# A list schedule's clock: other times from engine to engine, and a PSUM tile taken whole

## The chip, the cores and the metric

The kernel runs on one core of a Trainium2 chip. Five queues work side by side: PE (TensorE, matmuls and transposes), DVE (VectorE), ACT (ScalarE), POOL (GpSimd) and SP (which issues the DMAs). Each takes its instructions strictly in the order of the program; between queues only waits hold the order. The metric is device time in microseconds for one execution, lower is better. A time here is the median of several executions; the profile comes from one execution of its own.

## What is computed

Two sequences of 1024 positions and 128 channels go through four residual blocks, each behind a layer norm:

```python
x = x + mamba(_layernorm(x))       # selective state space, 256 inner channels, 16 states
x = x + experts(_layernorm(x))     # 8 experts, two picked one after the other, then a norm
x = x + encoder(_layernorm(x))     # 6 layers, below
x = x + fp4_ffn(_layernorm(x))     # gate, up, down with 4-bit blocks of 16
```

A layer of the encoder has 16 heads of 8 channels, and takes most of the time:

```python
scores = jnp.einsum('blhd,bmhd->bhlm', q, k) * inv_sqrt_d
w_avg = jax.nn.softmax(scores, axis=-1).mean(axis=1)           # mean over the heads
new_w = jax.nn.softmax(CSCALE * w_avg + rel[None], axis=-1)
sa = jnp.einsum('blm,bme->ble', new_w, h)
h1 = _ln(h + sa, l1w, l1b)
h2 = _ln(h1, l2w, l2b)
ff = jax.nn.relu(h2 @ w1.T + b1_) @ w2.T + b2_
return (_ln(h2 + ff, l3w, l3b), None)
```

## The kernel before

**The work.** Class `Front` holds the state space block and the experts, `Encoder` the six layers, `Last` the 4-bit block. In `Encoder.attention` a layer and a sequence are eight blocks of 128 query rows with 16 heads each, so 6 x 2 x 8 x 16 = 1536 heads in all. For one head, PE writes scores of 128 rows by 1024 keys into a PSUM tile `sc` (four matmuls, two on each half of the rows of the array), DVE takes their maximum (`nm`), ACT the exponential with its row sum (`e`, `z`). For four heads together DVE takes the reciprocals of the sums (`rz`), POOL multiplies each `e` by its own, and PE transposes `e` onto two PSUM accumulators (`acc0`, `acc1`; 16 small matmuls a head). After 16 heads ACT makes the second softmax (`prT`) from the accumulators, PE multiplies it with the hidden state (again in a tile `sc`), and DVE adds the residual into `r`.

There are three `sc` tiles of 128 x 1024 fp32 and fourteen `e` tiles. The same three `sc` tiles serve every other product of the encoder: the transposes before a projection, the projection, and the feed-forward part. `Encoder.between` does what lies between two attentions, for half a sequence (512 rows) at a time, so 24 calls. Its first feed-forward product is 512 hidden units by 512 rows: two `sc` tiles, each filled in two halves of 512 columns, and after each half's matmul a relu on ACT reads that half. A matmul of this kind is two instructions in the trace. The second product (`w2T`) fills one more tile.

**The order.** Nothing runs while it is written down: `Recorder` passes each call to `Plan.record`, which keeps it as an `Op` with its engine, an estimated cost and the earlier operations that it depends on. These come from the boxes of the tiles that it reads and writes (`View.box`, a range in each dimension): two operations depend on each other where their boxes meet and one of them writes. Calls under `together` are one `Op`.

`Plan.schedule` is a list scheduler with a clock of its own. An operation is ready (`arrive`) when all that it depends on has ended, plus a hop where the other one is on another engine; where it needs a new tile, not before a tile has been free for `GAP`. In each round every engine takes, among its ready operations that could start within `PATIENCE` = 0.1 us of the soonest, the one of the lowest key; of these the earliest over all engines is placed. The keys are positions in the chain of heads. Scores have a key 40 heads ahead of their place, so PE prefers them wherever they can start in time. The work of `between` is spread over the heads of the attention behind it (`Work.spread`): an operation may not be placed before the heads have reached its `late`, and those that use a PSUM tile already taken carry the key of that tile's first user less 4.

The order of these placements is the order in which the program's instructions are written, so it is the order in each queue, SP's included. The waits between engines are put in afterwards by the framework, from the real tiles and the written order. The clock of the scheduler is not part of the program.

One thing besides the order comes from that clock: where PE stands still for more than `STILL` = 0.3 us while accumulators are open, pairs of matmuls on zeros are written into the gap, one for each `ZEROS` = 0.22 us of it.

The costs are figures in `Plan.estimate`: 1.09 us for an exponential with its sum, 0.07 + 0.00104 a column for a maximum (1.135 us), 0.44 for the scores of a head, 0.50 for its 16 transposes.

Of the kernel before, what the change touches and what calls it, by code (L numbers as in the profile page):

```python
# [16 lines left out]
PSUM = bass.MemoryType.PSUM  # L17
# [80 lines left out]
class View:  # L98
# [23 lines left out]
    def rearrange(self, *args, **kw):  # L122
        return self._then("rearrange", *args, **kw)

    def of(self, n):

        return View(self.buf, self.chain, self.box, n)
# [93 lines left out]
def meet(a, b):  # L221
    return all(x[0] < y[1] and y[0] < x[1] for x, y in zip(a, b))
# [9 lines left out]
class Plan:  # L232
# [1 line left out]

    GAP = 0.06
    SWITCH = 0.12

    def __init__(self, nc):  # L240
# [14 lines left out]
    def record(self, engine, fn, name, args, kw):  # L255
        if self.group is not None and self.group.calls:
            o = self.group
            assert o.engine == engine
        else:
            o = self.group or Op()  # L260
            o.engine, o.calls, o.cost, o.deps, o.bufs = engine, [], 0.0, set(), []
            o.key, o.late, o.locks, o.rows = self.key + self.ahead, self.late, False, 128
            o.pos, o.sums = self.key, None
            o.i, o.start, o.after, o.landing = len(self.ops), None, [], 0.0
            self.ops.append(o)
        o.calls.append((fn, args, kw))
        outs = [args[0]] if args else [kw["out"]]
        if not isinstance(outs[0], View):
            outs = []
        ins = list(args[1:]) + [v for k, v in kw.items() if k not in ("out", "accum_out")]  # L270
        if "accum_out" in kw:
            outs.append(kw["accum_out"])
        outs = [v for v in outs if isinstance(v, View)]
        ins = [v for v in ins if isinstance(v, View)]
        for v in ins:
            o.deps.update(d for box, d, w in v.buf.touched if w and meet(box, v.box))
        for v in outs:
            o.deps.update(d for box, d, w in v.buf.touched if meet(box, v.box))
        for v in ins:
            v.buf.touched.append((v.box, o, False))  # L280
        for v in outs:
            covers = lambda x: all(a[0] <= b[0] and b[1] <= a[1] for a, b in zip(v.box, x[0]))
            v.buf.touched = [x for x in v.buf.touched if x[1] is o or not covers(x)]
            v.buf.touched.append((v.box, o, True))
        o.deps.discard(o)
        for v in outs + ins:
            if v.buf not in o.bufs:
                o.bufs.append(v.buf)
                v.buf.uses += 1
        self.estimate(o, engine, name, args, kw, outs, ins)  # L290
        return o
# [114 lines left out]
    def schedule(self, regions):  # L406
# [17 lines left out]
        def arrive(o):  # L424
            t = 0.0
            for d in o.deps:
                if d.engine == "SP":
                    x = d.end + d.landing
                elif d.engine != o.engine:
                    x = d.end + self.GAP + (0.13 if d.engine == "PE" else 0.05)  # L430
                else:
                    x = d.end
                t = max(t, x)
            o.ready = t
            ready[o.engine].append(o)

        for o in ops:
            if not o.waits:
                arrive(o)
        heads = [o for o in ops if o.late is None and o.engine != "SP"]  # L440
        front = 0
        n, moved, sums = 0, 0.0, ()
        while n < len(ops):
# [5 lines left out]
            for e in engines:  # L449
                found, soonest = [], None  # L450
                for o in ready[e]:
# [4 lines left out]
                    for b in o.bufs:  # L456
                        if b.at is None:
                            s = b.slots
                            if not s.free or s.ordered and s.bufs[0] is not b:
                                ok = False  # L460
                                break
                            t = max(t, min(s.free)[0] + self.GAP)
                    if not ok:
# [8 lines left out]
                if not found:  # L472
                    continue
                t, o = min(
                    ((t, o) for t, o in found if t <= soonest + self.PATIENCE),
                    key=lambda x: (x[1].key, x[1].i),
                )
# [3 lines left out]
            t, o = best  # L481
# [29 lines left out]
            for x in o.after:  # L511
                x.waits -= 1
                if not x.waits:
                    arrive(x)
        for r in regions:
            r.open()
        for o in order:
# [9 lines left out]
            else:  # L527
                self.issue(o)

    PATIENCE = 0.1  # L530
    STILL = 0.3
    ZEROS = 0.22
# [1445 lines left out]
```

## Time and profile before

| | |
|---|---|
| median of 3 runs | 3137.64 us (3136.42 to 3147.6) |
| the profiled execution's own time | 3140.7 us |
| its span, first to last instruction | 3138.9 us |
| mean granted TensorE clock | 0.962 |
| scores, maxima and exponentials of the encoder | from about 433 to 2995 us |
| exponentials (ACT) | 1536 of 1115 ns, plus 198 ns to read the sum (overlapping) |
| maxima (DVE) | 1536 of 1213 ns |
| scaling of `e` (POOL) | 1536 of 1122 ns |
| scores (PE) | 6144 matmuls |
| zero matmuls (PE) | 1518, 229.8 us |

In the profile a line of the timeline has a start, a length, the engine, the operation, the tile that it writes and those that it reads, how many were merged into the line, and in brackets how long the engine stood idle before it and who ended that wait. Lengths of matmuls are modelled, and overlap the next ones. A line of the waits has the waiting engine and tile, the one that ended the wait, the total in us, the number of waits and the longest. In the view by stretches each engine has its busy time and its instructions, and behind them stand the granted TensorE clock, the DMA engines' busy share and GB/s. All instructions have the same source line, that of the helper that issues them, so groups go by tile.

### The profile page before, as it was taken

What the parts mean: (1) busy time and instruction counts of PE and PEld (TensorE: products, weight loads), DVE (VectorE), ACT (ScalarE), POOL (GpSimd) and SP (SyncE); (2) the same over time, 40 slices, a digit from 0 to 9 for tenths busy, and PEclk for the clock granted to TensorE, in tenths of its full rate; (3) what the DMA queues carried; (4) which work ended last, traced back from release to release, by engine and by line L of the source; (5) the groups of instructions that cost most, each with busy time, mean ns of one, the idle gap of its engine ahead of it and who ended that gap; (6) DMA issues with size and microseconds to landing.
All of it is one profiled execution on the core that took longest, in us unless ns stands there. A gap on an engine that the chain in (4) does not pass through costs nothing.

```text
span 3138.9 us, 92400 instructions
## 1 busy us (share of the span) xinstructions
PE 2855.5 (91%) x38448; PEld 1940.4 (62%) x38448; DVE 2333.2 (74%) x3462; ACT 2486.8 (79%) x4461; POOL 2538.2 (81%) x2886
## 2 busy tenths in 40 slices
PE   6699999999999999999999999999999998999965
PEld 3455444566666666666666766666667666666643
DVE  4777533588778878787787877877777778778867
ACT  5577556688889888898888888888888888779843
POOL 5888634588889898898898988989898799788845
PEclk8699999999999999999999999999999999999986
DMA  4233321023032231221322303223023132220000
GB/s 137 99 108 110 88 69 39 23 62 86 25 85 55 61 95 29 73 68 45 79 55 62 77 25 95 59 55 85 25 72 82 30 81 55 51 63 25 17 3 12
DMA packets 209427, 193.42 MB, mean 62 GB/s; under 512 B 127778, under 2 KB 174446, under 8 KB 205550
## 3 DMA queue, kind: packets, MB, share of 16 engines
q1 hardware_dynamic: 209006, 187.51, 22.9%
q8 instruction: 300, 4.92, 0.7%
q14 instruction: 121, 0.99, 0.1%
HBM read 129.52 MB, written 57.93 MB: 60 GB/s over the span
## 4 chain that ended last, share of the span: by engine, by line
PE 47%; ACT 22%; DVE 13%; issue 4%; POOL 3%; DMA 1%; SPq 0%; DVEq 0%; ACTq 0%; POOLq 0%
PE sc L404 26%; ACT e L404 16%; PE acc L404 14%; DVE nm L404 9%; PE ps L404 3%; PE po L404 3%; ACT prT L404 2%; POOL e L404 2%; ACT r L404 2%; PE acc L524 1%; DVE st L404 1%; DVE fh L404 1%; DVE r L404 1%; DMA k<-d_k 1%; ACT ff L404 1%
## 5 line engine op out<-in xcount | busy, mean ns | idle before, releaser
L404 DVE TENSOR_REDUCE nm<-sc 128x1 f32<-128x1024 f32 x1536 | 1800.3, 1213 | 439.6 <-PE sc L404 400.3
L404 POOL TENSOR_SCALAR e<-e,rz 128x1024 f32<-128x1024 f32 x1536 | 1690.9, 1122 | 267.9 <-DVE rz L404 262.7
L404 ACT ACTIVATE e<-sc,nm 128x1024 f32<-128x1024 f32 x1536 | 1704.6, 1115 | 212.1 <-DVE nm L404 137.5
L404 PEld LDWEIGHTS acc<-ident,e 64*128 64x128 f32 x24576 | 973.2, 141 | 207.4 <-POOL e L404 39.0
L404 PE MATMUL sc<-k,q 36*128 36x512 bf16 x6144 | 914.5, 380 | 85.1 <-ACT e L404 58.4
L404 PE MATMUL acc<-ident,e 64*128 64x64 f32 x24576 | 984.0, 225 | 6.7 <-issue 5.4
L404 PEld LDWEIGHTS <-q 36*128 36x128 bf16 x6144 | 301.2, 96 | 361.7 <-issue 275.7
L404 ACT ACTIVATION_READ_ACCUMULATOR e<-sc,nm 128x1 f32 x1536 | 304.6, 198 | 0.0
L524 PE MATMUL acc<-zeros 64*128 64x512 bf16 x1518 | 229.8, 379 | 0.0
L404 PE MATMUL sc<-hn,prT 128*128 128x129 f32 x1536 | 203.3, 286 | 7.7 <-ACT e L404 5.9
L404 PEld LDWEIGHTS sc<-hn,prT 128*128 128x128 f32 x1536 | 184.9, 196 | 27.8 <-ACT e L404 19.9
L404 ACT ACTIVATE h<-ps,b 128x512 f32<-128x512 f32 x128 | 87.5, 685 | 97.9 <-PE ps L404 97.6
L404 POOL TENSOR_TENSOR db<-dtx,bb 128x512 f32<-128x512 f32 x128 | 160.1, 1272 | 1.7 <-DVE hh L404 1.2
L404 PE MATMUL po<-h,m_w 128*128 128x512 f32 x256 | 139.6, 633 | 7.2 <-ACT h L404 6.5
L404 ACT ACTIVATE prT<-acc,zero 128x512 f32<-128x512 f32 x192 | 121.3, 683 | 14.3 <-PE sc L404 8.6
L404 ACT ACTIVATE da<-dt,zero,na 128x512 f32<-128x512 f32 x128 | 99.0, 779 | 40.1 <-DVE hh L404 38.1
L524 PEld LDWEIGHTS <-zeros 64*128 64x128 bf16 x1518 | 83.7, 96 | 73.5 <-issue 12.5
L404 PE MATMUL acc<-ident,rel 64*128 64x64 f32 x1536 | 87.3, 235 | 41.7 <-ACT prT L404 40.4
L404 PEld LDWEIGHTS acc<-ident,rel 64*128 64x128 f32 x1536 | 69.2, 143 | 78.9 <-ACT prT L404 70.5
L404 POOL TENSOR_TENSOR qk<-qk,part 128x512 f32<-128x512 f32 x96 | 111.2, 1159 | 8.0
L404 PE MATMUL ys<-ident,yc 128*128 128x128 f32 x512 | 82.3, 303 | 31.8 <-DVE yc L404 17.5
L404 POOL CAST part<-qk 128x512 bf16<-128x512 f32 x144 | 87.8, 610 | 28.8 <-ACT qk L404 23.3
(311 smaller groups left out, 2690.9 us busy)
## 6 DMA issues: line engine op xcount, KB each, us to landing
q<-d_q SPq DMA_DIRECT2D x192, 288.0 KB
bb<-bcd SPq DMA_DIRECT2D x128, 256.0 KB
k<-d_k SPq DMA_DIRECT2D x96, 288.0 KB
d_q<-part SPq DMA_DIRECT2D x192, 128.0 KB
d_k<-part SPq DMA_DIRECT2D x192, 128.0 KB
raw<-in_L_attn_W SPq DMA_DIRECT2D x12, 256.0 KB
d_q<-part SPq DMA_DIRECT2D x48, 64.0 KB
d_k<-part SPq DMA_DIRECT2D x48, 64.0 KB
```

What stands on the lines that cost most here:

```text
L404: fn(*[look(a) for a in args], **{k: look(v) for k, v in kw.items()})
L524: self.nc.tensor.matmul(out.real(), *zeros, start=False, stop=False, skip_group_check=True)
```

## The change

Three times of the scheduler's clock become others, and one rule of its dependencies.

| | before | after |
|---|---|---|
| from an operation on PE to one on another engine | 0.06 + 0.13 = 0.19 us | `FROM_PE` = 0.27 us |
| between any other two engines | 0.06 + 0.05 = 0.11 us | `HOP` = 0.16 us |
| from a tile's last use to its next owner | `GAP` = 0.06 us | `GAP` = 0.165 us |
| box of a PSUM tile in the dependencies | the columns touched | the whole tile |

`View.reach` gives the box of a tile in SBUF or DRAM, and the full shape for one in PSUM; `record` uses it in the place of `box` throughout. `PATIENCE`, `STILL`, `ZEROS`, the keys and all costs stay. The calls recorded are the same; what changes is the order in which they are written, and the number of zero matmuls, which follows from the gaps.

```diff
+    def reach(self):
+
+        if self.buf.space == "PSUM" and self.PSUM_AS_ONE:
+            return tuple((0, n) for n in self.buf.shape)
+        return self.box
+
+    PSUM_AS_ONE = True
...
-    GAP = 0.06
+    GAP = 0.165
     SWITCH = 0.12
...
         for v in ins:
-            o.deps.update(d for box, d, w in v.buf.touched if w and meet(box, v.box))
+            o.deps.update(d for box, d, w in v.buf.touched if w and meet(box, v.reach()))
         for v in outs:
-            o.deps.update(d for box, d, w in v.buf.touched if meet(box, v.box))
+            o.deps.update(d for box, d, w in v.buf.touched if meet(box, v.reach()))
         for v in ins:
-            v.buf.touched.append((v.box, o, False))
+            v.buf.touched.append((v.reach(), o, False))
         for v in outs:
-            covers = lambda x: all(a[0] <= b[0] and b[1] <= a[1] for a, b in zip(v.box, x[0]))
+            covers = lambda x: all(a[0] <= b[0] and b[1] <= a[1] for a, b in zip(v.reach(), x[0]))
             v.buf.touched = [x for x in v.buf.touched if x[1] is o or not covers(x)]
-            v.buf.touched.append((v.box, o, True))
+            v.buf.touched.append((v.reach(), o, True))
...
                 elif d.engine != o.engine:
-                    x = d.end + self.GAP + (0.13 if d.engine == "PE" else 0.05)
+                    x = d.end + (self.FROM_PE if d.engine == "PE" else self.HOP)
...
+    HOP, FROM_PE = 0.16, 0.27
     PATIENCE = 0.1
```

## The prediction

> **What bounds the kernel now.** First the page's busy times and slices, then the waits, then one feed-forward stretch of the timeline.
>
> ```profile
> PE 2855.5 (91%) x38448; PEld 1940.4 (62%) x38448; DVE 2333.2 (74%) x3462; ACT 2486.8 (79%) x4461; POOL 2538.2 (81%) x2886
> ...
> 433.00:2995.00 2562.00, 2403.50 (x36443) 1682.25 (x36443) 1976.23 (x2798) 2178.43 (x3953) 2155.51 (x2441) 0.99 0.23 57
> ```
>
> The second line is the encoder alone, from the view by stretches (PE, PEld, DVE, ACT, POOL; granted clock 0.99): 1536 heads in 2562 us, 1.67 us a head. ACT is busy 85% of it, POOL 84%, DVE 77%. PE's 94% holds 1518 matmuls on zeros (229.8 us) and work that only has to be in time. No engine is full; 384 us of ACT and 406 us of POOL are idle. So the time is set by how well the fixed orders of five queues mesh: by latency round a ring, PE scores into one of three `sc` tiles, DVE maximum, ACT exponential, tile free again. The list schedule decides those orders, by its own clock.
>
> ```profile
> DVE nm L404 <- PE sc L404: 400.3, 310, 21.4
> ...
> POOL e L404 <- DVE rz L404: 264.8, 136, 21.7
> ACT e L404 <- DVE nm L404: 137.5, 189, 3.2
> ...
> PE sc L404 <- ACT e L404: 82.1, 163, 1.5
> ```
>
> Those are total us, times and longest of the waits round the ring; their averages, 1.3, 1.9, 0.7 and 0.5 us, are many times a hop. The reader is to see that most are not hops but an operation that sits behind another one.
>
> ```profile
> 1507.13 1.11 ACT L404 ACTIVATE e<-sc,nm 128x1024 f32<-128x1024 f32 x1
> ...
> 1508.38 0.61 PE L404 MATMUL sc<-k,q 36*128 36x512 bf16 x4 [0.17 <-ACT e L404]
> ...
> 1511.02 0.61 PE L404 MATMUL sc<-k,q 36*128 36x512 bf16 x4 [0.18 <-ACT e L404]
> ...
> 1511.74 1.22 DVE L404 TENSOR_REDUCE nm<-sc 128x1 f32<-128x1024 f32 x1 [1.28 <-PE sc L404]
> ```
>
> Here one hop is read as the schedule counts it. ACT to PE: the exponential starts at 1507.13 and the scores that take its tile at 1508.38, 1.25 later; the schedule books 1.09 for the exponential, so the hop is 0.16 (old 0.06, new 0.165). PE to DVE: 1511.02 to 1511.74 is 0.72, the schedule books 0.44 for the four matmuls, hop 0.28 (old 0.19, new 0.27). In the chain of waits the maximum at 1337.16 is followed by its exponential at 1338.42: 1.26 less the 1.135 booked is 0.125 (old 0.11, new 0.16). So two of the new figures are right within 0.01, and the third is somewhat high.
>
> ```profile
> 815.42 1.12 PE L404 MATMUL sc<-hT,w1T 128*128 128x512 f32 x2
> ...
> 817.01 1.13 PE L404 MATMUL sc<-hT,w1T 128*128 128x512 f32 x2
> ...
> 818.18 1.26 ACT L404 ACTIVATE ff<-sc,e_b 128x512 f32<-128x512 f32 x2 [0.59 <-PE sc L404]
> ...
> 907.36 3.89 PE L404 MATMUL sc<-hT,w1T 128*128 128x512 f32 x8 [0.18 <-DVE r L404]
> ...
> 908.52 0.69 ACT L404 ACTIVATE ff<-sc,e_b 128x512 f32<-128x512 f32 x1 [1.37 <-PE sc L404]
> 909.26 0.30 PEld L404 LDWEIGHTS sc<-hT,w1T 128*128 128x128 f32 x2 [0.75 <-ACT ff L404]
> ```
>
> At 815 the first half of a tile is written by 816.54, ACT is free at 817.59, and its relu starts only at 818.18, 0.04 after the second half's matmul ends. At 909.26 the second half's weight load waits for the relu of the first half (908.52 + 0.69 = 909.21). Both directions wait for the tile, not for its half.
>
> **The change, part by part.** No instruction is added except zero matmuls, and none changes its cost; the sum is over waits, against the profiled execution's 3140.7 us (span 3138.9), which is 3.1 above the median 3137.64.
>
> *The PSUM tile as one.* It binds only where a tile is written again after a reader: the two halves of the feed-forward's `ps` in `between`, 24 calls of two tiles, 48 pairs. All other PSUM tiles are filled before they are read, or stay in one chain. Now the relu of the first half comes before the second matmul in the order. In 28 of 48 pairs of the trace the relu started 0.04 us after the second matmul; ACT's idle time that this made sums to 20.7 us. In the other 20 (the form at 907) the true order is already relu first. ACT has 15% slack to lose, so I count half: -10. The other side: the second matmul (two instructions, 1.13 us) cannot run beside the first relu, so a tile is held for 1.13 + 0.04 + 0.69 + 0.05 + 1.13 + 0.04 + 0.69 = 3.8 us at best, against a mean of 3.6 now (first matmul to last relu, 48 pairs). If an exponential (1.1) is ahead of the relu, PE stands at the second matmul with score matmuls queued behind it, and DVE waits for those. Bounds: 0, and 48 x 1.1 = 53 us. The row nearest is the 3.8, so 48 x 0.2 = 10 us of holding; the ring above is 0.72 + 1.26 + 1.25 = 3.23 us, so with two tiles instead of three it turns at 1.62 instead of 1.08 a head, one third lost: +3. Sum -7.
>
> [...]
>
> *The hops.* PE to others 0.19 to 0.27, other pairs 0.11 to 0.16, a freed tile 0.06 to 0.165. What the old clock does not see at the waits of the ring: 163 x 0.105 (PE for ACT) + 310 x 0.08 (DVE for PE) + 189 x 0.05 (ACT for DVE) + 136 x 0.05 (POOL for DVE) = 17 + 25 + 9 + 7 = 58 us. The true hop stays; what the new order can win is other ready work placed in it and an operation not booked ahead of one that is really first. Most gaps are shorter than the smallest filler (a Ln of 0.30 us), so not all 58. Ends: 58 won; and lost, by the second rival, about the same. I take four tenths, nearer to nothing than to all since the waits average 0.5 to 1.9 us and a hop error explains little of each: -23.
>
> *Zero matmuls.* A planned gap over 0.3 us on PE gets pairs at 0.22 us. Gaps grow by about 0.1, so gaps of 0.2 to 0.3 now pass. 759 pairs now; perhaps 200 more, 44 us on PE, which lie in PE's waits for tiles. Cover gone where such a wait is shorter than planned: one in ten, +4. The clock, at 0.99, has nothing to win. Bounds 0 and +44.
>
> *The rest.* SP's issues keep their cost and move with the work that feeds them; the queue mostly stands waiting for tiles to be freed, and the loads run one block of queries ahead, 16 heads at 1.67 us or 27 us, so a shift of 1 us is hidden: 0. The front (433 us) and the tail (144 us) are chains whose order hardly has a choice: 0, within 5 either way.
>
> Sum: -7 - 23 + 4 = -26, profile 3114.7; less 3.1, median 3112.
>
> **The rivals.** *No measurable change.* The pair gain (-10) and holding (+3) stand, the hops' order is absorbed by fourteen `e` tiles between ACT, POOL and PE: -7 + 4 gives 3135. For it: 15% idle everywhere and a decision window of 0.1 us that already blurs hops. Against: the twelve attentions (six layers by two sequences) take nearly the same order, so a small loss or gain comes twelve times.
>
> *Slower: scores behind transposes.* The old clock believes a freed tile usable 0.105 us too early, and so lets the scores go first while PE really waits. With the true hop the tile comes more than 0.1 us, the decision window, after PE is free, and a ready group of 16 transposes onto `acc` starts: 0.49 us (32 take 1.16, 16 take 0.67), so scores are 0.49 - 0.105 = 0.39 late and DVE and ACT with them. It decides from (26 / 0.39) 67 heads on; with 140 of 1536 heads it is 55 - 26 = +29: 3166. For it: ACT and PE waits that short are in the trace, 163 of them. Against: by these rows PE has 158 us of idle and 230 us of zeros, so the group would usually have run before.
>
> *The change does not do what it says:* halves that wait only for their own half would make the new edge false: 48 tiles held 0.69 + 0.16 longer, 41 us, one third lost is +14, the gain of 10 gone, -23 + 14 + 4 = -5: 3133. The two lines at 818 and 909 speak against it. [...]
>
> **How the numbers follow.** Faster as summed 0.49, slower by transposes 0.32, no change 0.15, false edge 0.04. A measurement of this kernel tells about 0.5% (16 us) from nothing. Both middle cases lie within it, so faster 0.49, same 0.19, slower 0.32. The range: low end, all 58 of the hops with the pairs, -7 - 58 = 3073; high end, the slower rival with a few more heads, 3172. The faster case's own range is 3073 to 3122.
>
> **What would show it.** Right: no relu of `ff` more than 0.1 us after its own matmul with ACT idle; DVE's wait for `sc` under 380 us; ACT and POOL busy above 86% in the encoder; more than 759 zero pairs. Wrong: DVE's wait for `sc` above 430 us with transposes just ahead of the scores; the feed-forward tile held over 4.2 us on average; or a row of POOL waiting for `rz` that grows.

## The result: a third of a per cent faster

| | median | runs | ratio to the kernel before, 95% interval |
|---|---|---|---|
| kernel before | 3143.15 us | 20 | 1 |
| changed kernel | 3131.34 us | 20 | 0.9965 (0.9952 to 0.9978) |

The forecast was 3112 us, 0.8% faster. The sign was right, the size was not: 11 us by the ratio, of 26, and, as the experiments show, not from the places that were named. Single executions of one kernel spread widely here (3118.65 to 3147.14 us for the changed one, 3130.31 to 3147.79 for the one before), so a difference of 10 us between two profiles says nothing by itself. The first profiled execution of the changed kernel was the slowest of its 20, at 3147.14 us. The lines below come from a second one (3132.47 us, experiment 7), 1 us from the median.

The busy times of the changed kernel, and the encoder alone in the view by stretches (PE, PEld, DVE, ACT, POOL, granted clock):

```profile
PE 2888.4 (92%) x38754; PEld 1933.9 (62%) x38754; DVE 2345.2 (75%) x3462; ACT 2488.2 (79%) x4461; POOL 2538.4 (81%) x2886
...
433.00:2995.00 2562.00, 2441.64 (x36887) 1677.59 (x36886) 1988.67 (x2809) 2178.30 (x3952) 2160.90 (x2449) 0.99 0.23 57
```

The reader is to see that ACT and POOL are no busier: ACT 2178.30 us of the same 2562, as against 2178.43, POOL 2160.90 for 2155.51. DVE has 12 us more. PE's 38 us more are zero matmuls (1824 for 1518, 268.9 us for 229.8).

The waits of the changed kernel (total us, times, longest):

```profile
DVE nm L412 <- PE sc L412: 326.6, 331, 4.4
...
POOL e L412 <- DVE rz L412: 215.2, 138, 22.4
ACT ny L412 <- DVE mvs L412: 142.3, 60, 9.3
ACT e L412 <- DVE nm L412: 135.9, 193, 3.3
...
DVE r L412 <- PE sc L412: 49.3, 23, 5.3
...
PE sc L412 <- ACT e L412: 45.2, 69, 3.5
POOL e L412 <- PE sc L412: 38.7, 18, 3.4
...
ACT ff L412 <- PE sc L412: 17.5, 39, 1.8
```

The same view of the kernel before, in the rows that the prediction did not show:

```profile
ACT ny L404 <- DVE mvs L404: 74.0, 53, 10.4
...
ACT ff L404 <- PE sc L404: 54.6, 66, 3.9
...
DVE r L404 <- PE sc L404: 6.9, 2, 5.3
```

Here something moved a great deal. DVE waits 74 us less for scores, POOL 50 us less for reciprocals, PE 37 us less for freed tiles, ACT 37 us less for the feed-forward's matmuls. Of DVE's 74 us, some 20 are only booked elsewhere: the one long wait of the first maximum (21.4 us before) is still there (20.0 us), but put down to ACT. Against the falls ACT waits 68 us more in front of `ny`, the logarithm of a norm's variance, DVE 42 us more in front of the residual `r`, POOL has a new wait of 38 us for PE, and PE's weight loads wait 36 us more for `e` from POOL (74.8 for 39.0). Taken from the first maximum to the last, ACT's idle time is 385, 391 and 382 us in three profiles of the old order (before, 8 and 5) and 390, 378 and 385 us in three of the new one (first, 7 and 6).

The timeline of one feed-forward tile and the norm behind it, changed kernel:

```profile
1425.42 1.12 PE L412 MATMUL sc<-hT,w1T 128*128 128x512 f32 x2
...
1426.59 0.69 ACT L412 ACTIVATE ff<-sc,e_b 128x512 f32<-128x512 f32 x1
...
1427.55 0.30 PEld L412 LDWEIGHTS sc<-hT,w1T 128*128 128x128 f32 x2 [0.42 <-ACT ff L412]
1427.55 1.12 PE L412 MATMUL sc<-hT,w1T 128*128 128x512 f32 x2
...
1428.72 0.69 ACT L412 ACTIVATE ff<-sc,e_b 128x512 f32<-128x512 f32 x1 [0.35 <-PE sc L412]
...
1440.12 3.84 PE L412 MATMUL sc<-w2T,ff 128*128 128x128 f32 x32
...
1444.07 0.69 DVE L412 TENSOR_TENSOR r<-sc,h2b 128x512 f32<-128x512 f32 x1 [1.32 <-PE sc L412]
...
1445.98 0.30 ACT L412 ACTIVATE ny<-mvs,eps 128x4 f32<-128x4 f32 x1 [3.44 <-DVE mvs L412]
```

The first relu now starts 0.05 us after its own matmul (1426.59 behind 1425.42 + 1.12), and not behind the second one. But the four groups of `w2T` follow each other on PE without scores between them, and ACT, which has `ny` next in its queue, stands for 3.44 us while PE, then DVE, finish the chain in front of it. In the kernel before, the scores of a head stood between the third and the fourth group:

```profile
1445.53 2.95 PE L404 MATMUL sc<-w2T,ff 128*128 128x128 f32 x24
...
1448.41 0.61 PE L404 MATMUL sc<-k,q 36*128 36x512 bf16 x4
...
1448.94 1.16 PE L404 MATMUL sc<-w2T,ff 128*128 128x128 f32 x8
...
1450.27 0.68 DVE L404 TENSOR_TENSOR r<-sc,h2b 128x512 f32<-128x512 f32 x1
...
1452.17 0.30 ACT L404 ACTIVATE ny<-mvs,eps 128x4 f32<-128x4 f32 x1 [0.52 <-DVE mvs L404]
```

Scores stand inside the `w2T` product in 22 of the 24 calls before and in none of the changed kernel. It is the whole tile that does it: with the new times alone they still do in 22 of the 24 (experiment 2), with the whole tile alone in none (1). The four groups write different columns of one tile, so by the columns touched they don't depend on each other; with the tile taken whole, each depends on the one before it.

**Where the 11 us are.** Starts of the 1st, 129th, 1281st and last maximum, from the trace of each profiled execution, in us:

| kernel | front | first attention | nine attentions | last two | tail | span |
|---|---|---|---|---|---|---|
| before | 431.6 | 290.4 | 1847.7 | 424.2 | 145.1 | 3138.9 |
| before, again (8) | 429.2 | 290.5 | 1855.0 | 424.2 | 149.2 | 3148.1 |
| before, more zeros (5) | 433.6 | 288.3 | 1844.8 | 427.6 | 145.2 | 3139.4 |
| changed | 427.6 | 287.4 | 1855.3 | 426.4 | 148.3 | 3145.0 |
| changed, again (7) | 426.6 | 285.8 | 1843.5 | 426.0 | 148.3 | 3130.3 |
| changed, fewer zeros (6) | 425.5 | 286.0 | 1855.0 | 422.7 | 148.3 | 3137.5 |

The nine attentions, where most of the 26 us was to come from, take 1849 us on the mean of the three profiles of the old order and 1851 in those of the new one. The front is 5 us shorter on the mean and the first attention 3, in every one of the three profiles of the new order; the last attentions and the tail together are 1 to 2 us longer. That is about 7 of the 11 us; the rest lies within the spread of the nine attentions (12 us between executions of one kernel) and isn't located. Why the front is shorter is open.

One comparison is finer. The traces record the granted clock as full or half (1.0 or 0.5, 28 records of each in the first profile of the kernel before), and a half of an attention (64 heads) without any time at half rate can be compared by itself. Among the nine attentions of the same six profiles, the second 64 heads then take 107.9 to 108.2 us in the old order and 108.7 to 109.0 in the new one; the first 64 take 94.5 to 97.0 and 93.5 to 97.7. So where the clock does not disturb it, the new order wins nothing and is 0.8 us slower in the second half.

### The profile page after: what moved, and what is told of

The parts are those of the page before. It is cut to its first block, busy times and chain, and to the rows that moved or that the text cites. A ratio compares the mean times of both kernels' runs of the same rounds, so it can differ in the third digit from the quotient of the medians.

```text
span 3145.0 us, 92936 instructions
## 1 busy us (share of the span) xinstructions
PE 2895.5 (92%) x38754; PEld 1937.9 (62%) x38754; DVE 2344.9 (75%) x3462; ACT 2489.1 (79%) x4461; POOL 2544.5 (81%) x2886
## 4 chain that ended last, share of the span: by engine, by line
PE 46%; ACT 18%; DVE 13%; POOL 8%; issue 4%; DMA 1%; SPq 0%; POOLq 0%; DVEq 0%; ACTq 0%
PE sc L412 25%; PE acc L412 14%; ACT e L412 13%; DVE nm L412 9%; POOL e L412 5%; PE ps L412 3%; PE po L412 3%; ACT prT L412 2%; PE acc L532 1%; ACT r L412 1%; DVE st L412 1%; DVE fh L412 1%; POOL h2b L412 1%; POOL qk L412 1%; DMA k<-d_k 1%
## 5 line engine op out<-in xcount | busy, mean ns | idle before, releaser
L412 PEld LDWEIGHTS acc<-ident,e 64*128 64x128 f32 x24576 | 953.6, 141 | 255.4 <-POOL e L412 75.6
L412 PEld LDWEIGHTS <-q 36*128 36x128 bf16 x6144 | 294.4, 96 | 329.8 <-issue 234.2
L532 PE MATMUL acc<-zeros 64*128 64x512 bf16 x1824 | 268.7, 376 | 0.0
L532 PEld LDWEIGHTS <-zeros 64*128 64x128 bf16 x1824 | 97.5, 95 | 87.7 <-issue 9.8
L412 ACT ACTIVATE ny<-mvs,eps 128x4 f32<-128x4 f32 x80 | 23.8, 298 | 142.4 <-DVE mvs L412 136.1
```

Source lines behind the costliest of these rows:

```text
L412: fn(*[look(a) for a in args], **{k: look(v) for k, v in kw.items()})
L532: self.nc.tensor.matmul(out.real(), *zeros, start=False, stop=False, skip_group_check=True)
```

## Experiments

Ratios are against the kernel before on the same chip, with 95% intervals.

**1 and 2: each half of the change alone.** 1 keeps the old times and takes PSUM tiles whole, 2 has the new times and the old boxes:

```diff
 # 1
-    GAP = 0.165
+    GAP = 0.06
-    HOP, FROM_PE = 0.16, 0.27
+    HOP, FROM_PE = 0.11, 0.19
 # 2
-    PSUM_AS_ONE = True
+    PSUM_AS_ONE = False
```

> Only the PSUM tile as one; hops and tile gap as before. Holding theory: a feed-forward tile is held about 0.8 us longer (4.4 for 3.6), a third of 48 x 0.8 is lost and the 10 us of the pairs balance it: ratio to the kernel before 0.999 to 1.002. The prediction's own term (-7 us): 0.998. Rival, the PSUM part carries the whole gain: 0.996 or less.

> Only the hops and the tile gap; dependencies by the columns touched, as before. If the hops carry the gain: 0.995 to 0.997, with DVE's wait for sc near the 336 us of the changed kernel and the feed-forward relus late again (idle before ff near 50 us). If the PSUM part carries it: 0.999 to 1.001, and DVE's wait near 400.

Measured: 1 is 1.0082 (1.0057 to 1.0107), 2 is 1.0026 (1.0006 to 1.0047). Neither half gains time; +26 and +8 us alone, -11 together. No expected ratio held. DVE's wait for `sc` in 2 is 398.9 us, which was expected for the case that the PSUM part carries the gain. The four waits of the ring that the prediction showed are 885 us together before (898 in 8), 908 in 2, 810 in 1, and 762 and 723 in the two profiles of the changed kernel: the new times alone do not lower them. In the waits of 1,

```profile
ACT ny L412 <- DVE mvs L412: 158.9, 64, 8.1
...
ACT ff L412 <- PE sc L412: 40.6, 40, 2.2
```

the wait before `ny` is there already, so it comes with the whole tile and not with the hops: in 2 it is 80.1 us. The same goes for DVE's wait before `r`, 67.5 us in 1 and 6.5 in 2. In 1 the feed-forward tiles are held for 4.4 us on the mean of 48 (3.6 before), as in the changed kernel, and its nine attentions take 1867.7 us. Second halves of an attention without half-rate time take 110.0 to 110.3 us in 1 and 107.3 in 2, for 107.9 to 108.2 before: there the new times do gain 0.8 us, and the first halves lose it again (95.6 to 99.1 us in 2). The tail of 1 is 161.1 us, 12 to 16 more than in the profiles of the old order, though none of its operations changed. So the two parts cannot be added, and each has effects far from the tiles that it concerns.

**3: without zero matmuls.** The changed kernel with `STILL = 99.0`, so that none is written; the order is unchanged.

> The changed kernel without any zero matmul (they add nothing to the sums, so nothing of the computation is left out); the order is otherwise the same. If zeros stand in PE's way (the prediction's +4 for 153 more pairs, so 20 to 25 for all 912): 0.988 to 0.990. If they lie wholly in waits: 0.996. If they are what holds the granted clock at 0.98 in the encoder: the clock falls, and the ratio is over 1.00.

Measured: 1.016 (1.0132 to 1.0189), 2% slower than the changed kernel. The middle stretch, here and in the changed kernel (experiment 7):

```profile
720.00:2550.00 1830.00, 1643.39 (x25651) 1175.09 (x25649) 1437.70 (x1982) 1575.04 (x2853) 1575.30 (x1778) 0.95 0.25 61
```

```profile
720.00:2550.00 1830.00, 1745.81 (x27291) 1222.50 (x27286) 1457.73 (x2018) 1604.42 (x2912) 1610.80 (x1818) 0.99 0.25 62
```

The granted clock falls from 0.99 to 0.95, and POOL does 1778 instructions in the stretch for 1818, 2% fewer. From the first maximum to the last the time at half rate is 304 us, for 65 in 7. The third expectation held: with the order unchanged, the clock is held by the zeros here, 0.99 with them and 0.95 without.

**4: all three times doubled** (0.54, 0.32, 0.33).

> The changed kernel with all three times doubled (0.54, 0.32, 0.33). If the true hop is the best clock: slower than the kernel before by 0.5 to 2%, since the plan then fills gaps that are not there and places scores late. If the order is not sensitive to the hop, and the gain was one draw among many orders: 0.993 to 1.003.

Measured: 1.0265 (1.0242 to 1.0288), the highest clock of all (0.971) and 1681 pairs of zeros. A clock that is far off does cost, in the one order tried, by more than was expected: PE's weight loads wait 248 us for `e` from POOL (39 before), which fits transposes that are booked too early in the queue.

**5 and 6: order or zeros.** The longer gaps bring 153 more pairs of zeros, and without any the clock fell from 0.99 to 0.95 (experiment 3); so 5 gives the old order more pairs (937 for 759), 6 the new order fewer (776 for 912):

```diff
 # 5, on the kernel before        # 6, on the changed kernel
-    ZEROS = 0.22                  -    ZEROS = 0.22
+    ZEROS = 0.20                  +    ZEROS = 0.27
```

> The kernel before with ZEROS = 0.20 instead of 0.22: the same order, 937 zero pairs instead of 759. If the changed kernel's gain comes from the zeros that its longer gaps let in (fewer stretches at half the granted clock): 0.994 to 0.998, and less half-rate time in the encoder. If it comes from the order: 1.000 to 1.003, the pairs standing in PE's way a little.

> The changed kernel with ZEROS = 0.27: its order, 776 zero pairs instead of 912, about as many as before. If the gain comes from the zeros: back to 1.000 to 1.004, with more half-rate time. If it comes from the order: 0.994 to 0.998 as the changed kernel.

Measured: 5 is 1.001 (0.9993 to 1.0027), 6 is 0.9958 (0.994 to 0.9976). The gain comes with the order; 23% more zeros or 15% fewer make no difference that can be told. Nor does the half-rate time between first and last maximum follow them: 72 us in 5 as in the kernel before, 61 in 6 for 65 in 7.

**7 and 8: both kernels once more.**

> The changed kernel once more, for a second profile and for times beside the others of this call: ratio 0.995 to 0.998. A stretch of 64 heads without half-rate time takes 94.6 to 95 us (heads 0 to 64 of an attention) and 108.8 to 109.1 us (64 to 128) if the first profile is typical, as against 94.2 to 94.7 and 108.2 to 108.4 before.

> The kernel before once more, for a second profile: ratio 0.998 to 1.002, the half-rate time of the encoder somewhere else but again near 72 us if it is a property of the order, and much different if chance.

Measured: 0.9966 (0.9953 to 0.998) and 0.9999 (0.998 to 1.0018). The gain is repeatable. Their profiles gave the table above. Halves without half-rate time take 94.8 to 95.4 and 108.8 to 109.0 us in 7, near what was expected, and 94.5 to 97.0 and 107.9 to 108.2 in 8. The half-rate time of 8 is 75 us for the 72 of the first profile, and mostly in the same places (last section).

**9, 10, 11: neighbours.** Times that differ by 0.01 us, less than two readings of one hop differ by in the trace (see below):

```diff
 # 9: FROM_PE, HOP, GAP = 0.26, 0.15, 0.155     10: 0.28, 0.17, 0.175
 # 11, on the kernel before
-    GAP = 0.06
+    GAP = 0.07
```

> The changed kernel with all three times 0.01 us less (0.26, 0.15, 0.155). If the gain is the worth of a true clock: 0.995 to 0.998, since 0.01 us is below what the trace tells. If each clock is a draw among orders: anywhere from 0.99 to 1.01, with the wait of ACT's ny and DVE's wait for sc both changed.

> The changed kernel with all three times 0.01 us more (0.28, 0.17, 0.175). Worth of a true clock: 0.995 to 0.998. Draw: anywhere from 0.99 to 1.01.

> The kernel before with GAP 0.07 for 0.06, so all three old times 0.01 us more. Worth of a true clock: 0.999 to 1.001. Draw: anywhere from 0.99 to 1.01.

Measured: 9 is 1.0045 (1.0028 to 1.0062), 10 is 0.9997 (0.9979 to 1.0016), 11 is 0.9997 (0.9978 to 1.0016). Between 0.26, 0.27 and 0.28 the ratio goes 1.0045, 0.9965, 0.9997. That is no trend, and the interval of 9 lies wholly above that of the changed kernel: the gain does not belong to the true hop. It is one draw among orders; these three, the kernel before and 11 lie within 0.8% of each other. Of the nine other orders in these experiments (1, 2, 4 and 9 to 14) none is faster than the kernel before and seven are slower, so that one was a good draw already. In the profile of 9 the front takes 435.9 us, 9 more than in the changed kernel, and the nine attentions 1859.6.

**12: true costs for fp32 matmuls.** In the trace 32 instructions of `w2T` take 3.84 us, where the schedule books 3.46; the new wait before `ny` could come from that.

```diff
-            t = n * (1 if bf else 2 if turn else 4) / 2400.0 + 0.003
+            t = n * (1 if bf else 2 if turn else 4.56) / 2400.0 + 0.003
```

> The changed kernel with the cost of fp32 matmuls raised by 14% (four w2T groups then cost 3.9 us, as the 3.84 of the trace, for 3.46). If the new wait of ACT's ny for the norm's statistics comes from this cost (the plan places ny 0.5 us and more too early): that wait falls from 136 us to under 90, and the ratio is 0.990 to 0.995. If it comes from the tile's dependencies alone: the wait stays over 120 and the ratio is 0.996 or more.

Measured: 1.0102 (1.0082 to 1.0122), and the wait stays:

```profile
ACT ny L412 <- DVE mvs L412: 138.1, 61, 6.4
```

So it does not come from the cost: wait and ratio are as the second case had them. The nine attentions take 1842.3 us, nearly as short as any; what is lost is at the ends, a front of 450.2 us (427 in the changed kernel) and a tail of 159.2 (148.3).

**13 and 14: the wait before `ny` taken away.** The plan takes `ny` as ready 2 us later, so that exponentials go ahead of it; 13 on the changed kernel, 14 on the one before:

```diff
-            o.ready = t
+            o.ready = t + o.lag          # 0.0 but for the norm's Ln and Exp
...
+        p.ops[-1].lag = 2.0              # in Encoder.norm, behind the two activations
```

> The changed kernel, where the plan takes the norm's Ln on ACT (ny) to be ready 2 us later than by its clock, so that exponentials are booked ahead of it. If the wait of ny (142 us in the second profile, 74 before) is what ate the hops' gain: that wait under 60 us, ratio to the kernel before 0.985 to 0.993. If ACT's idle time only moves on: wait under 60, ratio 0.995 to 1.005. If nothing can be put there: wait over 110.

> The same 2 us for ny in the kernel before. If the wait costs time wherever it stands: 0.993 to 0.997 (74 us to under 40). If idle time only moves on: 0.998 to 1.005.

Measured: 13 is 1.004 (1.0026 to 1.0054), as expected if idle time only moves on; 14 is 1.0125 (1.0108 to 1.0143), slower than either case, with the wait down from 74.0 to 23.5 us. The waits of 13:

```profile
ACT e L412 <- DVE nm L412: 248.2, 216, 5.2
...
POOL nr L412 <- ACT ny L412: 113.7, 39, 7.1
...
ACT ny L412 <- DVE mvs L412: 10.0, 4, 8.6
```

The wait before `ny` is gone, 10 us for 142. ACT's wait for maxima went from 136 to 248, POOL's for `ny` from 47 to 114, and the kernel became 0.7% slower than the changed one. Idle time was moved on and nothing was won: a wait that is taken away need not be time won. The test is not pure, as 13 and 14 are other orders throughout.

## Why the prediction was wrong

*The reading of the hops* rested on one pair of operations each. Over all such waits of the kernel before, scores start 1.24 to 1.28 us behind the exponential that frees their tile (143 of 144), which fits the 0.165. The maximum starts 0.64 to 0.66 us behind its scores in 102 of 312 cases and 0.70 to 0.75 in 178; less the 0.44 booked these are hops of 0.20 to 0.22 and 0.26 to 0.31. The exponential starts 1.23 to 1.30 us behind its maximum in 112 of 210 and 1.31 to 1.34 in 98; less 1.135 that is 0.10 to 0.17 and 0.18 to 0.21. So two readings of one hop differ by up to 0.1 us, and 0.27 and 0.16 are not the only figures that fit.

*The hops, -23 us*: this step failed. It took the time that the old clock does not see at the ring's waits (58 us) and counted four tenths of it as time won. The new times alone did not lower those waits (885 to 908 us, experiment 2) and cost 8 us. With both parts the ring's waits did fall, to 723 us, but the time of the nine attentions did not, 1849 and 1851. The time that went from these waits came back as idle time elsewhere: ACT, 85% busy in the encoder, is idle for 382 to 391 us in the old order and for 378 to 390 in the new. What does set the 1851 us was not found: in all orders but those with doubled times (4) and without zeros (3) it lay between 1841 and 1868.

*The PSUM tile, -10 and +3*: this step failed too, and by more: alone it is +26 us where -7 stood. The relu's wait is gone as said (ACT before `ff` 54.6 to 17.5). The price was not 0.2 but 0.8 us of holding a tile. And "it binds only" at the 48 pairs of halves was wrong: it also binds the four groups of `w2T`, which let scores in between before (22 of 24 calls) and no longer do (none). Behind them DVE's wait before `r` went from 6.9 to 49.3 us and ACT's before `ny` from 74.0 to 142.3; both rise with the whole tile alone and not with the times alone. How much of the 26 us this costs was not measured by itself. The prediction followed the chain to the second matmul, and should have followed it to its end.

*Adding the parts*: -7 and -23 were summed. Measured, +26 and +8 make -11. In a list schedule a term has no price of its own; each change makes another order of everything behind it. As each part alone has the other sign, that the sum had the right one is luck.

*Zero matmuls, +4*: 153 more pairs for the 200 guessed, and no cost that can be told from none: 178 more pairs are +3 us in 5, and 136 fewer are 3 us less in 6 than in 7, both within the intervals. "The clock has nothing to win" holds for more zeros, but without any 2% are lost (3).

*Front and tail, 0 within 5*: for this change about true, -5 and +2. As a statement on how much choice these chains have it was wrong: other orders of the same work make the front 450 us (12) and the tail 164 (14).

*The rivals.* None came as described. Scores behind transposes would have raised DVE's wait for `sc`, which fell. The false edge between halves is refuted by the lines at 818 and 909 and again at 1427.55, where the second half's weights wait 0.42 us for the first half's relu. "No measurable change" was given 3135 and was nearest in time, by 4 us. But its reason, an order that the buffers absorb, does not fit: the gain is clear of noise, and other orders cost about 1% (1, 12, 14).

*The signs that were named*: relus no longer late, DVE's wait under 380 us and more zero pairs all came true, while the two that speak of time did not (ACT and POOL above 86% busy: 85 and 84). A tile held over 4.2 us, named as a sign of the prediction being wrong, was there (4.4).

## What to carry to other kernels

Waits along a ring were no sum of time to be won here, where no engine is full (ACT 85% busy in the encoder, POOL 84%): take the busy share of the engines in the stretch as the test, and expect, as in experiment 13, that idle time may only move on. Before a rule of the dependencies is changed, list every tile that it binds, and not only the one that it is meant for. A change to a list schedule's clock is a draw of another order, here worth half a per cent either way; before a gain of that size is put down to its reason, run two neighbours with figures that differ by less than can be read from the trace, and each part alone. When several orders come this cheap, trying a handful and keeping the best one is a fair method, but what is kept then is an order, not a truth about the clock.

## What the runs showed of the hardware

That the kernel without zero matmuls takes 2% longer, at a clock of 0.95 for 0.99 (experiment 3), was more than expected, and so was that 23% more or 15% fewer of them are worth nothing that can be told.

The dips of the granted clock are not all chance. Three successive stretches of one half attention each, kernel before, first profile and second profile:

```profile
1952.00:2050.00 98.00, 91.83 (x1507) 66.19 (x1504) 79.37 (x106) 88.43 (x159) 90.09 (x97) 0.98 0.30 70
2050.00:2158.00 108.00, 101.84 (x1555) 72.63 (x1555) 83.39 (x122) 91.75 (x170) 90.36 (x109) 1.00 0.24 61
2158.00:2255.00 97.00, 90.47 (x1483) 65.04 (x1480) 79.00 (x106) 86.35 (x156) 89.46 (x96) 0.98 0.23 58
```

```profile
1958.00:2056.00 98.00, 91.47 (x1493) 65.64 (x1491) 79.25 (x106) 88.33 (x160) 90.09 (x97) 0.98 0.30 68
2056.00:2164.00 108.00, 102.00 (x1567) 72.90 (x1565) 83.38 (x122) 91.78 (x170) 90.09 (x108) 1.00 0.25 62
2164.00:2261.00 97.00, 90.08 (x1473) 65.27 (x1469) 78.90 (x105) 86.26 (x157) 89.52 (x95) 0.98 0.23 57
```

Both executions dip to 0.98 in the same two stretches and stay at 1.00 in the same one. By the clock records of the traces, the time at half rate is equal in 19 of the 24 half attentions of these two executions and in 17 of those of the changed kernel's two, but only in 6 to 10 between an execution of one kernel and one of the other. So the dips go in the main with the order of the work, and a part of them changes from one execution to the next. That part makes most of the spread: of the 11.8 us by which the nine attentions of the changed kernel's two executions differ, 9.5 lie in the five half attentions whose half-rate time differs. How much of the difference between two orders comes from where their dips fall was not tested by itself.
